# A GRU followed by an expert-choice layer: states in a ring with one gather, another load order, and softmax and late sums arranged anew

## The chip, the core and the metric

The kernel runs on one core of a Trainium2 chip. A core has five engines that work side by side: TensorE (PE) for matmuls, with its weight loads (PEld) shown apart, VectorE (DVE), ScalarE (ACT), GpSimd (POOL) and SyncE (SP). Sixteen DMA engines move data between the large memory (HBM) and the on-chip memory (SBUF). Matmuls write into PSUM, which has eight banks of 128 partitions by 512 float32 values. The metric is the time of one execution on the device in microseconds (us); lower is better.

## The reference

Inputs are `x` (16 x 256 x 512, float32), a start state `cond` (16 x 512), two GRU weight matrices of 512 x 1536 with biases, a router of 512 x 16 and an expert of 512 x 512 with their biases. First a GRU runs over 256 steps, then an expert-choice layer routes each of the 16 x 256 = 4096 tokens, and the result is added to `x`:

```python
def cell(h, x):
    gi = x @ W_ih + b_ih
    gh = h @ W_hh + b_hh
    i_r, i_z, i_n = jnp.split(gi, 3, axis=-1)
    h_r, h_z, h_n = jnp.split(gh, 3, axis=-1)
    r = jax.nn.sigmoid(i_r + h_r)
    z = jax.nn.sigmoid(i_z + h_z)
    n = jnp.tanh(i_n + r * h_n)
    return (1.0 - z) * n + z * h
...
logits = xf @ router_w + router_b          # xf: the GRU's states, 4096 x 512
S = jax.nn.softmax(logits, axis=-1)
G, idx = jax.lax.top_k(S.T, k)             # k = 4096 / 16 = 256 tokens per expert
out = jnp.einsum('ekh,hd->ekd', xf[idx], expert_w) + expert_b
# each token's weighted expert outputs are summed, and x + y is returned
```

All 16 experts share one weight matrix, so a token's result is (state @ expert_w + expert_b) times one number, its gate: the sum of the probabilities with which experts chose it.

## The kernel before, in words

**Units.** Eight steps form a group (`TG = 8`; eight steps of 16 batch rows are 128 tokens), so there are 32 groups (`NG`). Two steps form a pair. A feature vector of 512 is cut into four blocks (`KC = 4`), and a matmul's output into four quadrants of 32 partitions, so a product is issued as four matmuls side by side. The trace counts each float32 matmul twice.

**Head.** Small loads (biases, router bias, start state) and the weights are issued on two queues, SP and ACT, in an order written by hand (L198 to L221, under `manual_schedule`): biases first, then `xa0` (x of group 0), the start state `c0`, then `wih` r and n, `whh` r and n, `wih` z, `whh` z, each in two halves of 512 KB, one on each queue, then `xa1` (x of group 1), the expert and router weights `ewr`, the expert bias `eb` and the router bias `rb`. PE first zeroes six PSUM banks (`begin_sums`, L119) and adds the biases (L236); then come the x products of pair 0 (`x_part`, L337): `ra` holds r and the x side of n, `zz` holds z, `hn` the state side of n, each in two copies for alternate pairs. DVE turns x around (`turn_x`, L190).

**Recurrence.** For the 256 steps the order on all five engines is the written one (L372). In a step PE adds the state products for r, n and z (`h_part`, L350), then part of the x products of the next pair (three of four blocks of `ra` in an even step, the last block and all of `zz` in an odd one). ACT takes the sigmoid of r (L407), the two tanh halves (L428) and the sigmoid of z (L429); DVE multiplies and adds (L424, L426), transposes n and z (L433, L436), and forms the new state in two halves: `less_n` (L439), `by_z` (L444), `plus_n` (L447). States go into `hs`, which has a place for each of the 257. After a group, POOL copies its states into token order (`gather`, L267, into `tok`, two buffers). For every second group PE then computes logits and expert sums in small units between the steps (`expert`, L303), and DVE adds the bias and writes the sums over the states of that group in `hs` (`expert_done`, L320). For the 17 others (`late_groups`) only the logits are computed in the recurrence (`logits`, L280). Logits less their maximum go into `lg` (`less_max`, L273, L274). POOL also makes two small copies a step or fewer (L106, L472), which hold back the SP queue's next loads of x until a step is reached.

**Tail.** After the last group's logits: exp, sum, reciprocal and product over all groups (L546 to L550), four transposes on PE (L556), a copy (L560), then a search for each expert's 256th largest probability in 30 bits: DVE compares and counts (L572), PE adds the counts (L577), DVE sets the bit (L580, L583). PE fills its time with the late groups' expert sums (`expert_for`, L519), two or three of 136 parts a bit. For a late group POOL gathers the states again (`late_begin`, L498), ACT writes the bias into a PSUM bank (L503), PE adds eight parts, and ACT copies the sums over the group's states (L531). After the search come ranks among equals (L594 to L630), the gates (L633, L635), and for each of the 32 groups one DVE operation, x plus gate times sums (L641), and a 256 KB store on SP (L644); the late groups are last.

## Time and profile before

Three runs took 1204.85, 1210.37 and 1207.17 us; their median is 1207.17 us.

| what | value |
|---|---|
| median of three runs | 1207.17 us |
| the profiled execution's own time | 1206.09 us |
| its span, first to last instruction | 1204.2 us |
| mean granted TensorE clock | 0.993 |
| PE, PEld, DVE, ACT, POOL busy | 96%, 86%, 58%, 27%, 11% |
| moved by DMA | 38.05 MB, of it 28.90 MB on the busiest queue |
| first step's r sigmoid | at 28.61 us |
| step 1's first state product | at 30.95 us |
| last step's state complete | at about 1108.4 us |
| search begins, ends | at 1116.7, 1161.2 us |
| gates ready, first output product | at 1169.5 us |
| last output product begins | at 1199.8 us |

Times in the profile count from the span's start. A line of a group, such as those quoted in the prediction, names the line of the kernel, the engine, the operation, the tile written and the tiles read, the shapes and the number of instructions; in a list in order of time the first column is the start and the second the length, and in brackets stands how long the engine had been idle and what released it. A line of the table by stage has the stretch, its length, the busy time of each engine with its instruction count, the granted clock (1.00 is full), the DMA engines' busy share and what they moved in GB/s. A line of waits names who waited for whom, the total in us, how often, and the longest.

### The profile page before, as it was taken

Reading aid. Unit: us, or ns where it says so; the run is one execution under the profiler, and the core shown is the slowest. Engines: PE = TensorE matmul, PEld = TensorE weight load, DVE = VectorE, ACT = ScalarE, POOL = GpSimd, SP = SyncE. Lnnn points to the kernel's source line nnn. Section 1 sums busy time; section 2 is a strip of 40 time slices with the busy share of each in tenths; the row PEclk is TensorE's granted clock in tenths of the full one; section 3 lists DMA queues with packets and bytes.
Section 4 is the critical chain, followed back from the end, with each engine's and each line's share of the span. In section 5 each row is a group of like instructions: output and inputs, shape, how many; then the busy total and the mean of one; then the engine's idle time right before and its main releaser. Section 6 shows DMA issues by size and latency. Waiting matters only on the chain.

```text
span 1204.2 us, 80862 instructions
## 1 busy us (share of the span) xinstructions
PE 1161.5 (96%) x36482; PEld 1041.2 (86%) x36482; DVE 703.2 (58%) x3915; ACT 327.6 (27%) x1440; POOL 131.7 (11%) x458
## 2 busy tenths in 40 slices
PE   4999999999999999999999999999999999998896
PEld 3899999999999899999999999999999999996443
DVE  1555655565555655565655655555655655565685
ACT  0223232222222222222322222222222232223221
POOL 0000000000000000000000000000000000002235
PEclk9999999999999999999999999999999999999998
DMA  7100000000000000000000000000000000000007
GB/s 260 36 21 21 20 18 22 19 20 20 20 22 20 20 19 20 20 22 20 20 21 19 20 20 19 20 22 20 18 22 20 20 19 21 20 11 8 2 29 253
DMA packets 48833, 38.05 MB, mean 32 GB/s; under 512 B 7909, under 2 KB 40677, under 8 KB 48488
## 3 DMA queue, kind: packets, MB, share of 16 engines
q1 hardware_dynamic: 45364, 28.90, 8.1%
q8 instruction: 285, 4.67, 1.5%
q10 hardware_dynamic: 3124, 3.98, 1.0%
q14 instruction: 60, 0.49, 0.1%
HBM read 24.47 MB, written 8.39 MB: 27 GB/s over the span
## 4 chain that ended last, share of the span: by engine, by line
PE 88%; DVE 6%; DMA 2%; POOL 1%; issue 1%; ACT 1%; ACTq 0%; DVEq 0%; POOLq 0%
PE ra L350 19%; PE hn L350 19%; PE zz L350 17%; PE ra L337 16%; PE zz L337 9%; PE pe L303 4%; PE pe L519 3%; POOL tok L498 1%; DVE ge L572 1%; DVE nT L433 1%; DMA whh<-in_L_cond_W_hh_dram 1%; DVE t L424 1%; DMA xa<-in_x_dram 1%; DVE zT L436 1%; ACT n L428 1%
## 5 line engine op out<-in xcount | busy, mean ns | idle before, releaser
L350 PE MATMUL ra<-whh,hs 128*16 128x128 f32 (+1 forms) x8192 | 338.2, 273 | 6.5 <-DVE zT L436 5.1
L350 PE MATMUL hn<-whh,hs 128*16 128x128 f32 (+1 forms) x8192 | 337.5, 273 | 0.8 <-DMA whh<-in_L_cond_W_hh_dram 0.8
L424 DVE TENSOR_TENSOR t<-r,hn 128x64 f32<-128x64 f32 x512 | 90.5, 218 | 370.3 <-PE hn L350 349.2
L337 PE MATMUL ra<-wih,xt 128*32 128x256 f32 x4096 | 281.9, 381 | 5.8 <-DMA wih<-in_L_cond_W_ih_dram 4.4
L350 PE MATMUL zz<-whh,hs 128*16 128x128 f32 (+1 forms) x8192 | 281.4, 273 | 2.2 <-DMA whh<-in_L_cond_W_hh_dram 1.8
L350 PEld LDWEIGHTS ra<-whh,hs 128*16 128x16 f32 (+1 forms) x8192 | 237.2, 103 | 18.6 <-issue 7.6
L350 PEld LDWEIGHTS hn<-whh,hs 128*16 128x16 f32 (+1 forms) x8192 | 249.9, 103 | 1.4 <-DMA whh<-in_L_cond_W_hh_dram 1.3
L350 PEld LDWEIGHTS zz<-whh,hs 128*16 128x16 f32 (+1 forms) x8192 | 235.8, 103 | 4.2 <-DMA whh<-in_L_cond_W_hh_dram 2.1
L407 ACT ACTIVATE r<-ra 128x128 f32<-128x128 f32 x256 | 71.2, 278 | 580.1 <-PE ra L350 580.1
L337 PEld LDWEIGHTS ra<-wih,xt 128*32 128x32 f32 x4096 | 149.5, 110 | 41.1 <-issue 9.6
L428 ACT ACTIVATE n<-t 128x64 f32<-128x64 f32 x512 | 104.1, 250 | 192.9 <-DVE t L426 192.6
L337 PE MATMUL zz<-wih,xt 128*32 128x128 f32 x4096 | 142.6, 273 | 1.7 <-DMA wih<-in_L_cond_W_ih_dram 1.2
L337 PEld LDWEIGHTS zz<-wih,xt 128*32 128x32 f32 x4096 | 125.7, 110 | 18.4 <-issue 2.4
L433 DVE STREAM_TRANSPOSE nT<-n 128x64 f32<-128x64 f32 x512 | 100.8, 235 | 57.5 <-ACT n L428 57.2
L436 DVE STREAM_TRANSPOSE zT<-zs 128x64 f32<-128x64 f32 x512 | 122.0, 238 | 0.9 <-ACT zs L429 0.6
L447 DVE TENSOR_TENSOR hs<-v,nT 128x32 f32<-128x32 f32 x512 | 102.1, 199 | 17.5
L444 DVE TENSOR_TENSOR v<-u,zT 128x32 f32<-128x32 f32 x512 | 105.7, 206 | 8.8
L303 PE MATMUL pe<-ewr,tok 128*32 128x136 f32 (+1 forms) x1920 | 103.0, 276 | 0.0
L426 DVE TENSOR_TENSOR t<-t,ra 128x64 f32<-128x64 f32 x512 | 88.9, 216 | 0.1
L303 PEld LDWEIGHTS pe<-ewr,tok 128*32 128x32 f32 x1920 | 70.9, 110 | 12.8
L439 DVE TENSOR_TENSOR u<-hs,nT 128x32 f32<-128x32 f32 x512 | 78.6, 154 | 0.0
L519 PE MATMUL pe<-ewr,tok 128*32 128x256 f32 x1088 | 71.2, 406 | 5.3 <-POOL tok L498 5.3
(100 smaller groups left out, 553.4 us busy)
## 6 DMA issues: line engine op xcount, KB each, us to landing
xs<-in_x_dram SPq DMA_DIRECT2D x128, 64.0 KB, 2.2
out_dram<-xs SPq DMA_DIRECT2D x32, 256.0 KB, 3.6
xa<-in_x_dram SPq DMA_DIRECT2D x248, 32.0 KB, 2.2
wih<-in_L_cond_W_ih_dram ACTq DMA_DIRECT2D x3, 512.0 KB
wih<-in_L_cond_W_ih_dram SPq DMA_DIRECT2D x3, 512.0 KB
whh<-in_L_cond_W_hh_dram ACTq DMA_DIRECT2D x3, 512.0 KB, 11.5
whh<-in_L_cond_W_hh_dram SPq DMA_DIRECT2D x3, 512.0 KB, 12.2
ewr<-in_L_ffn_expert_w_dram ACTq DMA_DIRECT2D x1, 512.0 KB, 4.0
```

What stands on the lines that cost most here:

```text
L303: nc.tensor.matmul(pe[quadrant(j), at : at + w], toks[g][:, k, quadrant(j)], ewr[:, k, src : src + w], start=(k == 0), stop=(k == KC - 1), ...
L337: nc.tensor.matmul(dst, lhs, rhs, start=False, stop=(k == KC - 1), tile_position=(0, QD * j), skip_group_check=True)
L350: nc.tensor.matmul(dst[quadrant(j, m)], lhs, columns(whh[:, k, slot, :], j), start=False, stop=(k == KC - 1), tile_position=(0, QD * j), s ...
L424: nc.vector.tensor_tensor(t[half], r[:, cols], hn[p % 2][:, cols], ALU.mult)
L426: nc.vector.tensor_tensor(t[half], t[half], ra[p % 2][:, 1, cols], ALU.add)
L428: nc.scalar.activation(n[half], t[half], AF.Tanh)
L433: nc.vector.transpose(nT[half], n[half])
L436: nc.vector.transpose(zT[half], zs[:, halves[half][1]])
L439: nc.vector.tensor_tensor(u[half], hs[:, halves[half][2], s, :], of_step(nT[half], odd), ALU.subtract)
L444: nc.vector.tensor_tensor(v[half], u[half], of_step(zT[half], odd), ALU.mult)
L447: nc.vector.tensor_tensor(hs[:, halves[half][2], s + 1, :], v[half], of_step(nT[half], odd), ALU.add)
L519: nc.tensor.matmul(pe[q, cols], tok[:, k, q], ewr[:, k, E:][:, cols], start=False, stop=(k == KC - 1), tile_position=(0, QD * j), skip_gro ...
```

## The change

- **States in a ring.** `hs` shrinks to the start state and 16 places, used in turn (`slot`). A new tile `ht` holds the token order of all 32 groups; `gather` writes into it once, and the logits, the expert units and the late sums all read it. Expert sums are written over a group's part of `ht` (`wide`).
- **Head.** Biases, router bias and the start state are loaded from POOL's queue. SP and ACT begin with `wih` r, then `xa0`, `wih` n, `wih` z, then all of `whh`. `xa1` and everything after it goes on SP alone. The x products of pairs 0 and 1 are all issued before step 0, so steps 0 and 1 issue none.
- **Softmax.** exp, sum, reciprocal and product of groups 0 to 30 are issued before those of group 31. The fourth transpose goes into a bank of its own, and its copy is DVE's.
- **Late sums.** The first two late groups' banks are begun in steps 250 and 252, the others after the fifth part of the group two before. Four parts follow the last logits directly. Five banks are used in turn instead of three. Sums that are complete before the gates are copied by ACT as before; later ones are read by the output product from PSUM. PE's remaining parts are issued between the output products instead of ahead of them.

The diff, cut to its core (`late_part` is the body of L519's matmuls with `ht` in place of `tok`; in the remaining places `toks` becomes `ht` and `s` becomes `slot(s)`):

```diff
--- before.py
+++ after.py
@@ -60,12 +64,13 @@
     const = ctx.enter_context(tc.tile_pool(name="const", bufs=1))

     xs = const.tile([P, NG, D], F32, name="xs")
-    hs = const.tile([P, KC, T + 1, B], F32, name="hs")
+    ht = const.tile([P, NG, KC, P], F32, name="ht")
     HD = D // 2
...
+    tot = const.tile([P, NG], F32, name="tot")
...
-    def load_x(g, j, s):
-
-        cols = slice(j * P, (j + 1) * P)
-        nc.gpsimd.tensor_copy(xs[0:1, g, cols][:, 0:1], hs[0:1, 0, s, 0:1])
-        nc.sync.dma_start(out=xs[:, g, cols], in_=x[:, g * TG : (g + 1) * TG, cols])
-
-    def expert_out(g):
-        return hs[:, :, g * TG + 1 : (g + 1) * TG + 1, :].rearrange("p k t b -> p k (t b)")
-
-    def blocks(ap):
-        return ap.rearrange("p (k d) -> p k d", d=P)
...
+    def wide(g):
+
+        return ht[:, g, :, :].rearrange("p k d -> p (k d)")
+
+    ps_m = ctx.enter_context(tc.tile_pool(name="ps_m", bufs=2, space=bass.MemoryType.PSUM))
+
...
+    late = []
+    late_sums = {}
+    late_done = []
+    gated = []
+
+    def late_begin(pool, fresh=True):
+        g = late_groups[len(late_done) + len(late)]
+        pe = pool.tile([P, D], F32, name="pe", tag="pe")
+        if fresh:
+            begin_sums(pe)
+        nc.scalar.copy(pe, eb)
+        late.append((g, pe))
+
+    def late_parts():
+        for i, g in enumerate(late_groups):
+            _, pe = late[0]
+            for part in range(2 * KC):
+                late_part(g, pe, part)
+                if part == KC and i + 2 < len(late_groups):
+                    n = (i + 2) % 5
+                    late_begin(ps_m if n < 2 else late_pool[0], fresh=i < 3)
+                if part == 2 * KC - 1:
+                    late.pop(0)
+                    late_done.append(g)
+                    if gated:
+                        late_sums[g] = pe
+                    else:
+                        nc.scalar.copy(wide(g), pe)
+                yield
...
-        tc.tile_pool(name="toks", bufs=2) as tp,
+        tc.tile_pool(name="states", bufs=1) as sp,
         tc.tile_pool(name="ps_g", bufs=1, space=bass.MemoryType.PSUM) as ps_g,
-        tc.tile_pool(name="ps_m", bufs=1, space=bass.MemoryType.PSUM) as ps_m,
+        hs = sp.tile([P, KC, 2 * TG + 1, B], F32, name="hs")
+
+        def slot(s):
+            return 1 + (s - 1) % (2 * TG) if s else 0
...
         queues = (nc.sync, nc.scalar)
         ET = mybir.EngineType
         xa0 = new_xa()
+        for dst, src in (
+            (b_raw[0:1], b_ih.rearrange("(o g d) -> o g d", o=1, d=D)),
+            (b_raw[1:2], b_hh.rearrange("(o g d) -> o g d", o=1, d=D)),
+            (b_n, b_hh[2 * D :].rearrange("(o d) -> o d", o=1)),
+            (b_r, router_b.rearrange("(o e) -> o e", o=1)),
+        ):
+            nc.gpsimd.dma_start(out=dst, in_=src)
+        for j in range(KC):
+            nc.gpsimd.dma_start(
+                out=c0[QD * j : QD * j + B, :].rearrange("b (c i) -> b c i", c=KC), in_=columns(cond, j)
+            )
+        xa1 = new_xa()
         with tc.manual_schedule(engines={ET.SP, ET.Activation}):
-            for h, src in enumerate((b_ih, b_hh)):
-                queues[h].dma_start(out=b_raw[h : h + 1], in_=src.rearrange("(o g d) -> o g d", o=1, d=D))
-            nc.sync.dma_start(out=b_n, in_=b_hh[2 * D :].rearrange("(o d) -> o d", o=1))
-            nc.scalar.dma_start(out=b_r, in_=router_b.rearrange("(o e) -> o e", o=1))
+            for i, gate in enumerate((0, 2, 1)):
+                load_rows(wih[:, :, i, :], w_ih[:, gate * D : (gate + 1) * D], "(p c) n -> p c n")
+                if i == 0:
+                    for j in range(KC):
+                        load_xa(0, xa0, j, queues)
+            for gate in (0, 2, 1):
+                load_rows(whh[:, :, gate, :], w_hh[:, gate * D : (gate + 1) * D], "(c p) n -> p c n")
             for j in range(KC):
-                load_xa(0, xa0, j, queues)
-            for j in range(KC):
-                queues[j % 2].dma_start(
-                    out=c0[QD * j : QD * j + B, :].rearrange("b (c i) -> b c i", c=KC), in_=columns(cond, j)
-                )
-            for slot, gate in enumerate((0, 2, 1)):
-                if slot == 2:
-                    for h_gate in (0, 2):
-                        load_rows(whh[:, :, h_gate, :], w_hh[:, h_gate * D : (h_gate + 1) * D], "(c p) n -> p c n")
-                load_rows(wih[:, :, slot, :], w_ih[:, gate * D : (gate + 1) * D], "(p c) n -> p c n")
-            load_rows(whh[:, :, 1, :], w_hh[:, D : 2 * D], "(c p) n -> p c n")
-            xa1 = new_xa()
-            for j in range(KC):
-                load_xa(1, xa1, j, queues)
-            load_rows(ewr[:, :, E:], expert_w, "(c p) n -> p c n")
-            load_rows(ewr[:, :, 0:E], router_w, "(c p) n -> p c n")
+                load_xa(1, xa1, j, (nc.sync, nc.sync))
+            nc.sync.dma_start(out=ewr[:, :, E:], in_=expert_w.rearrange("(c p) n -> p c n", c=KC))
+            nc.sync.dma_start(out=ewr[:, :, 0:E], in_=router_w.rearrange("(c p) n -> p c n", c=KC))
             nc.sync.dma_start(out=eb, in_=expert_b.rearrange("(o d) -> o d", o=1).to_broadcast([P, D]))
-            nc.scalar.dma_start(out=rb, in_=router_b.rearrange("(o e) -> o e", o=1).to_broadcast([P, E]))
+            nc.sync.dma_start(out=rb, in_=router_b.rearrange("(o e) -> o e", o=1).to_broadcast([P, E]))
...
         def gather(g):

-            toks[g] = tp.tile([P, KC, P], F32, name="tok")
             n = TG - 1 if g == NG - 1 else TG
+            at = slot(g * TG + 1)
             for k in range(KC):
                 nc.gpsimd.tensor_copy(
-                    toks[g][:, k, :].rearrange("p (b t) -> p b t", t=TG)[:, :, 0:n], tokens(g, k)[:, :, 0:n]
+                    ht[:, g, k, :].rearrange("p (b t) -> p b t", t=TG)[:, :, 0:n],
+                    hs[:, k, at : at + n, :].rearrange("p t b -> p b t"),
                 )
...
-                pes[g] = [ps_m.tile([P, n], F32, name=f"pe{n}") for n in (E + HD, HD)]
+                pes[g] = [ps_m.tile([P, D], F32, name="pe", tag="pe")[:, 0:n] for n in (E + HD, HD)]
...
-                out_h = expert_out(g)[:, KC // 2 * h : KC // 2 * (h + 1), :]
-                nc.vector.tensor_tensor(out_h, blocks(pe if h else pe[:, E:]), blocks(eb[:, d]), ALU.add)
+                nc.vector.tensor_tensor(wide(g)[:, d], pe if h else pe[:, E:], eb[:, d], ALU.add)
...
-                lhs = hs[:, k, s - odd : s + 1, :].rearrange("p t b -> p (t b)")
+                lhs = hs[:, k, slot(s) - odd : slot(s) + 1, :].rearrange("p t b -> p (t b)")
...
-        for k in range(KC):
-            x_part(0, k, False)
+        for z in (False, True):
+            for p in range(2):
+                for k in range(KC):
+                    x_part(p, k, z)
...
-                if s == 0:
-                    for k in range(KC):
-                        x_part(0, k, True)
                 h_part(s, "z", range(KC))
...
-                if s + 2 < T:
+                if 2 <= s < T - 2:
...
-                        hs[:, halves[half][2], s + 1, :], v[half], of_step(nT[half], odd), ALU.add
+                        hs[:, halves[half][2], slot(s + 1), :], v[half], of_step(nT[half], odd), ALU.add
...
+                if s in (T - 6, T - 4):
+                    late_begin(ps_m)
+
+
+            old, new = slice(0, NG - 1), slice(NG - 1, NG)
+
+            def softmax(gs):
+                nc.vector.reciprocal(tot[:, gs], tot[:, gs])
+                n = gs.stop - gs.start
+                nc.vector.tensor_tensor(
+                    lg[:, :, gs], lg[:, :, gs], tot[:, gs].unsqueeze(1).to_broadcast([P, E, n]), ALU.mult
+                )
+
+            def exp_sum(gs):
+                nc.scalar.activation(lg[:, :, gs], lg[:, :, gs], AF.Exp)
+                nc.vector.tensor_reduce(tot[:, gs], lg[:, :, gs].rearrange("p e g -> p g e"), AX.X, ALU.add)
+
             nc.vector.tensor_copy(
-                toks[NG - 1].rearrange("p k (b t) -> p k b t", t=TG)[:, :, :, TG - 1], hs[:, :, T, :]
+                ht[:, NG - 1, :, :].rearrange("p k (b t) -> p k b t", t=TG)[:, :, :, TG - 1], hs[:, :, slot(T), :]
             )
             logits(NG - 1, hn[(T // 2) % 2][:, P:])
+            expert_for(4)
+            exp_sum(old)
             less_max(NG - 1, hn[(T // 2) % 2][:, P:])
+            softmax(old)
+            exp_sum(new)
+            softmax(new)
...
-        def late_begin(g):
-
-
-            tok = lt.tile([P, KC, P], F32, name="tok")
-            for k in range(KC):
-                nc.gpsimd.tensor_copy(
-                    tok[:, k, :].rearrange("p (b t) -> p b t", t=TG),
-                    hs[:, k, g * TG + 1 : (g + 1) * TG + 1, :].rearrange("p t b -> p b t"),
-                )
-            pe = ps_e.tile([P, D], F32, name="pe")
-            nc.scalar.copy(pe, eb)
-            return tok, pe
...
-
-            for _ in range(3):
-                begin_sums(ps_e.tile([P, D], F32, name="pe"))
-            ready = [late_begin(g) for g in late_groups[:2]]
-            for i, g in enumerate(late_groups):
-                tok, pe = ready.pop(0)
...
-                    if part == 3 and i + 2 < len(late_groups):
-                        ready.append(late_begin(late_groups[i + 2]))
-                    if part == 2 * KC - 1:
-                        nc.scalar.copy(expert_out(g), blocks(pe))
-                    yield g
...
+        late_pool.append(ps_e)
...
-        sm = rt.tile([P, E, NG], F32, name="sm")
-        nc.scalar.activation(sm, lg, AF.Exp)
-        tot = rt.tile([P, NG], F32, name="tot")
-        nc.vector.tensor_reduce(tot, sm.rearrange("p e g -> p g e"), AX.X, ALU.add)
-        nc.vector.reciprocal(tot, tot)
-        nc.vector.tensor_tensor(sm, sm, tot.unsqueeze(1).to_broadcast([P, E, NG]), ALU.mult)
-
-        expert_for(4)
         ps = ps_s.tile([P, QG, P], F32, name="ps", tag="s")
-        sm_f = sm.rearrange("p e g -> p (e g)")
-        for q in range(QG):
-            nc.tensor.transpose(ps[:, q, :], sm_f[:, q :: QG], ident)
+        ps_last = ps_n.tile([P, P], F32, name="ps_last", tag="n")
+        lg_f = lg.rearrange("p e g -> p (e g)")
         sT = rt.tile([P, QG * P], F32, name="sT")
+        for q in range(QG - 1):
+            nc.tensor.transpose(ps[:, q, :], lg_f[:, q :: QG], ident)
+        nc.tensor.transpose(ps_last, lg_f[:, QG - 1 :: QG], ident)
         by_row = lambda ap: ap.rearrange("p (q b t) -> p b q t", q=QG, b=B)
         by_step = lambda ap: ap.rearrange("p b (q t) -> p b q t", q=QG)
-        nc.scalar.copy(sT, ps.rearrange("p q n -> p (q n)"))
+        nc.scalar.copy(sT[:, 0 : (QG - 1) * P], ps[:, 0 : QG - 1, :].rearrange("p q n -> p (q n)"))
+        nc.vector.tensor_copy(sT[:, (QG - 1) * P :], ps_last)
...
-        expert_for(len(late_groups) * KC * 2)
+        gated.append(True)
         for g in [g for g in range(NG) if g not in late_groups] + late_groups:
+            while g in late_groups and g not in late_done:
+                expert_for(1)
             nc.vector.scalar_tensor_tensor(
-                blocks(xs[:, g, :]), expert_out(g), gate[:, g : g + 1], blocks(xs[:, g, :]), ALU.mult, ALU.add
+                xs[:, g, :], late_sums.get(g, wide(g)), gate[:, g : g + 1], xs[:, g, :], ALU.mult, ALU.add
```

## The prediction

> **What bounds the kernel now.** I read the page's busy shares first, then a table of busy time by stage, then each stage that is not steady in order of time, with the chain of waits beside it. The page and the stage table (us, busy time by engine, granted clock, DMA share, GB/s):
>
> ```profile
> PE 1161.5 (96%) x36482; PEld 1041.2 (86%) x36482; DVE 703.2 (58%) x3915; ACT 327.6 (27%) x1440; POOL 131.7 (11%) x458
> ...
> 0.00:31.00 31.00, 14.41 (x292) 10.13 (x296) 6.17 (x29) 2.13 (x5) 1.91 (x14) 1.00 0.77 259
> 31.00:1103.00 1072.00, 1066.07 (x34920) 988.56 (x34920) 628.76 (x3692) 302.21 (x1394) 88.05 (x371) 1.00 0.07 20
> ...
> 1117.00:1161.00 44.00, 39.81 (x622) 19.03 (x625) 32.53 (x119) 10.61 (x18) 12.83 (x36) 1.00 0.01 2
> 1161.00:1169.00 8.00, 7.26 (x107) 4.34 (x100) 7.27 (x18) 2.35 (x4) 3.68 (x8) 1.00 0.01 3
> 1169.00:1204.00 35.00, 24.66 (x378) 13.32 (x378) 21.66 (x33) 5.30 (x9) 17.83 (x8) 0.85 0.74 241
> ```
>
> PE is busy 1066 of the recurrence's 1072 us. The diff takes no matmul out of steps 2 to 255, so this block stays; what can move is 31 us of head and 101 of tail. Head, in order of time, and the SP queue's own waits:
>
> ```profile
> 16.93 8.68 ACTq L180 DMA_DIRECT2D xa<-in_x_dram  x4
> 26.07 1.07 PE L350 MATMUL zz<-whh,hs 128*16 128x128 f32 x32 [1.79 <-DMA whh<-in_L_cond_W_hh_dram]
> 27.31 1.28 ACT L407 ACT_TABLE_LOAD   x1 [27.31 <-DMA xa<-in_x_dram]
> 30.95 0.65 PE L350 MATMUL ra<-whh,hs 128*32 128x128 f32 x16 [2.52 <-DVE zT L436]
> ...
> SPq L180 <- DMA whh<-in_L_cond_W_hh_dram: 7.0, 3, 2.5
> SPq L172 <- DMA wih<-in_L_cond_W_ih_dram: 6.5, 2, 3.9
> SPq L180 <- DMA wih<-in_L_cond_W_ih_dram: 2.4, 1, 2.4
> SPq L180 <- DMA xs<-in_L_cond_b_ih_dram: 0.7, 1, 0.7
> ```
>
> Two things end the head: the last weights (z of whh) at 26.07, and ACT, which still issues xa1 and later loads until 27.3, so that step 0's sigmoid comes at 28.6 and step 1 at 30.95. The four waits fit one reading: over both queues, in written order, a load waits for the one eight places before it (xa0's third pair for b_ih; z of wih for r of wih; the four pairs of xa1 for whh r, whh n, wih z, whh z). Tail:
>
> ```profile
> 1111.63 3.64 PE L519 MATMUL pe<-ewr,tok 128*32 128x256 f32 x32
> 1116.68 0.75 DVE L572 TENSOR_SCALAR_CACHE_REDUCE ge<-sT,cand 128x512 bf16<-128x512 f32 x1 [3.74 <-ACT sT L560]
> ...
> 1169.53 19.96 DVE L641 SCALAR_TENSOR_TENSOR xs<-hs,gate,xs 128x512 f32<-128x512 f32 x30
> 1174.27 17.83 POOL L498 COPY tok<-hs 128x128 f32<-128x128 f32 x8 [5.60 <-PE pe L519]
> 1189.80 9.19 PE L519 MATMUL pe<-ewr,tok 128*32 128x256 f32 x128 [5.33 <-POOL tok L498]
> 1199.77 0.75 DVE L641 SCALAR_TENSOR_TENSOR xs<-hs,gate,xs 128x512 f32<-128x512 f32 x1 [2.73 <-ACT hs L531]
> ...
> 1194.00:1196.00 2.00, 2.00 (x40) 1.08 (x36) 0.00 (x0) 0.33 (x1) 0.00 (x0) 0.98 1.00 348
> 1196.00:1198.00 2.00, 2.00 (x44) 1.12 (x40) 0.75 (x1) 0.26 (x1) 0.00 (x0) 1.00 0.10 37
> ```
>
> At the end eight POOL gathers take 17.8 us (one alone 15.48) while DVE runs the 30 output steps; PE waits for them, the last two groups come at 1196.3 and 1199.8, and the DMA engines, full until 1196, fall to 0.10. So the output is bound by DMA for 30 groups and by the gathers for the last two.
>
> **The change part by part.** The sum is made against the profiled execution: span 1204.2, its own time 1206.09 (1.9 around the span). The median of the three runs is 1207.17, so 1.08 is added at the end.
>
> *Head.* New order on SP and ACT: wih r (places 0, 1), xa0 (2 to 9), wih n, wih z, whh r, n, z; all of xa1 and the later loads on SP alone. Wih r goes out at 0.74 instead of 5.2. It lands 4.1 to 5.3 us after its issue now (the loads that wait for it go out at 9.31 and 10.78), so at 4.9 to 6.0. By the rule of eight, xa0's last pair (places 8, 9) must wait for that, and wih n stands behind it on both queues: issue at about 6.3, with 1.25 MB alone in flight before, which leaves the engines a gap of 2 us. From there five MB: now six take 20.7 us from first issue to sight (26.07 less 5.4), and one is 2.7 to 2.9 (20.48, 23.19, 26.07 for the last three), so 17.9, and whh z is there at 24.2. Its matmuls take 1.07 and from the z sigmoid to step 1's first matmul it is 1.20 (29.75 to 30.95): step 1 at 26.5, gain 4.4. ACT's last issue waits for wih n, near 11.5, so its table load is done by 14 and hides. SP's eight xa1 issues, ewr, eb and rb end near 26; x of group 1 is needed at step 3, ewr at step 8 (30 us later), so nothing waits.
>
> The x products of pair 1 move from steps 0 and 1 into the head. They save nothing in step 1, which DVE bounds (30.95 to 35.04, with the next `ra` held by L447). In the head PE must do biases 3.9 (6.86 to 10.7), pair 0's `ra` 3.64 (15.15), pair 1's at full rate 1.74 (8 matmuls in 0.43), both z 2.2: 11.4 in all, from DVE's `ones`, which stand behind xa0's transpose (8.4 landing + 1.1): 9.5 to 20.9, before whh n at 21.4. Cover 0.5, plus 1.5 that the n side has on z; later biases cost one for one beyond 2 us.
>
> No row shows a DMA on POOL. Bounds: SP's small issues at 0.22 to 0.43 us with 2.1 to landing, against the Trainium skill, "DMA: Bandwidth & Descriptors", specifications, first byte about 1 us from GpSimd and 0.6 from SP or ACT. Four bias loads from 2.15 (POOL's last memset) land at 5 to 8.3, the four of the state at 7 to 12.3; I take 6.5 and 9, nearer the rows. Both are hidden. The same page ("Issuing engines are not separate DMA queues") speaks against the edit: spreading loads over engines saves only issue time, small beside the transfer. The trace disagrees here: between 2 and 6 us the DMA share is 0.15 to 0.48 and both queues issue without a break. By the rule whh z would still come at 26.07 and only ACT's early release count: step 1 at 28.3 (26.07 + 1.07 + 1.20), gain 2.6; by the row 4.4. I take the row, and keep 2 to 6.
>
> *Recurrence.* The gathers were all made once already (128 copies, L267) and only change their target; `expert_done` writes the same sizes. L444 to L447 gain one thing: a state overwrites a slot that POOL read up to 15 steps before. That event lies 60 us back, and the wait stands on an instruction that has none: zT of half 0 also waits on ACT and starts 0.07 after `u`, the same pace. Cost 0; bounds in the rivals. If POOL were late, DVE's second half and PE's next `ra` would queue behind it; its gather ends 1.6 us into a step, eight steps ahead. Two `begin_sums` (1.47 for three, cold) enter steps 250 and 252: at most 0.3 in all; their ACT copies (0.59) fit in the 1.7 us that ACT waits for `ra`.
>
> *Before the search.* Now: logits end at 1109.55, zeroing 1.47, four parts 3.6, transposes 0.8, copy 0.6, search at 1116.68. After: the parts follow the logits directly (1109.6 to 1113.1, same cold clock), transposes to 1113.95, the split copy 0.3 more: 1114.3. Gain 2.4. DVE is not late: reduce 1.04 from 1108.8 (table load and exp end by 1108.6), max and subtract 0.45, reciprocal 0.35, product 0.73, the new group's three small ones 0.6: 1112.0. Should PE get its full clock, 1112 becomes the bound.
>
> *Search.* Three zeroings move here: in bits with three parts (PE 1.48 of 1.47) they cost 0.25 to 0.5, in bits with two nothing: +0.6. POOL's copies go; they stretch L583 from 160 to 186 ns on average, 29 times: -0.5 of 0.76, as PE bounds half the bits. The clock: it is 0.50 from 1109.0 to 1115.5 and 1.00 from the search on. By that row, nothing. But the Trainium skill, "TensorE: Matmul & The Clock Gate", Part 1, says a free-running window of about 3.4 us must be busy before the clock rises; now 3.5 us of parts and 0.8 of transposes lie before a pause of 1.1, where zeroing and parts made 5.8. By the rule two or three bits may run cold, each three-part one 1.2 longer: 0 to 3. I take +1.2.
>
> *After the search.* `at_least` (0.93) runs beside a POOL copy, others of its kind 0.67 to 0.75: -0.3.
>
> *Output.* First bytes come 2.0 after the gates (1169.5 to 1171.5). 30 groups, 7.86 MB, went in 24.4 us, 322 GB/s; 32 need 26.1; data end 1197.8, plus the 1.2 that now lies between the last data and the end: 1199.0 against 1204.2, gain 5.2. Hidden under it: DVE 32 x 0.67; PE's 47 parts, seven cold in 4.9 and 40 at 0.43, to 1191.4. Six groups are read from PSUM (89 parts are done at the gates, 11 groups, which ACT copies as before); group 16 reuses the bank of group 11, free after DVE's 27th step at 1187.5, copy 0.6, eight parts 3.5, last product 1192.4; DMA reaches it at 1196.7. Cover 4; the ACT copies saved are worth nothing there.
>
> Sum: -4.4 +0.3 -2.4 +0.6 -0.5 +1.2 -0.3 -5.2 = -10.7: 1195.4 for a run like the profiled, 1196.5 beside the median.
>
> **The rivals.** *A: the head keeps its length.* POOL's loads count among the eight places, or land after 13 us: PE then ends its x products past 24. For it: no row; against: 3 us of cover. Gain 0.5: 1200.4. *B: the output stays late.* Bank reuse behind DVE and a cold PE (0.54 at 1170 to 1172) hold the last groups past 1196.7; this takes 4 us, 40 parts at 0.53. Gain 2: 1199.7. *C, slower: the ring's wait costs a step of DVE's queue.* An instruction with two waits shows 0.10 ahead of it in the chain (37.02 to 37.12). On 254 steps 25 us, net 1222; break-even at 0.042 per step, or 0.084 if only every second step, the one that DVE bounds, pays. Against: one wait, not two. That the change does less than it says: only six of 17 late sums stay in PSUM; counted.
>
> **How the numbers follow.** Main 0.72 (1196.5; own range 1191.5 to 1200.5: head 2 to 6, search 0 to 3, output 4 to 6); A 0.15; B 0.08; C 0.05. Within 0.5% (6 us, about what a measurement here can tell from no change) are two fifths of A and B. Faster 0.86, same 0.09, slower 0.05. The range, 1191 to 1201.5, leaves out C, the ends of the main case and part of A.
>
> **What would show it.** Step 1's first `ra` at 26 to 27 and ACT's table load before 15 (A: past 29); whh z's wait ending near 24; pairs without expert units still 8.2 us (C: 8.3 to 8.4); search 2.4 earlier after the recurrence, its first bits longer than 1.5; no POOL copy after it; DMA full without a break for 26 us, and the last product 4 us ahead of the last data. A pair that grows, or biases after 11.5, would prove me wrong.

## The result, and the profile after

The changed kernel takes 1205.6 us (median of 20 runs, 1200.8 to 1209.1), the kernel before 1211.7 on the same chips (20 runs, 1204.9 to 1216.2): ratio 0.9947, 95% interval 0.9933 to 0.9961. The forecast was 1196.5, with a range to 1201.5. It is faster by 0.5%, 6 us where 10.7 were worked out, and from a base that was itself 4.5 too low: the three runs of before that were at hand (median 1207.17) lay in the lower half of what it does. The profiled execution of the changed kernel took 1205.67 (span 1203.9).

Of the page and of a table by stage (us, busy time of PE, PEld, DVE, ACT, POOL, granted clock, DMA share, GB/s):

```profile
PE 1163.5 (97%) x36490; PEld 1052.9 (87%) x36490; DVE 699.1 (58%) x3919; ACT 323.3 (27%) x1435; POOL 96.0 (8%) x398
...
0.00:31.00 31.00, 17.12 (x364) 12.29 (x368) 6.14 (x30) 2.24 (x5) 6.04 (x22) 0.96 0.71 236
...
1119.00:1165.00 46.00, 41.88 (x628) 19.72 (x626) 32.18 (x120) 10.97 (x20) 0.00 (x0) 0.96 0.01 2
...
1173.00:1204.00 31.00, 21.95 (x372) 12.43 (x364) 21.25 (x32) 0.72 (x2) 0.00 (x0) 0.87 0.84 273
```

POOL has no copy left in the search and the output, and the output takes 31 us in place of 34.7 with the DMA engines at 0.84. The head has more PE work (17.1 against 14.4) at a clock of 0.96. In order of time, with the SP queue's own waits and the clock of step 1:

```profile
3.42 0.48 ACTq L228 DMA_DIRECT2D wih<-in_L_cond_W_ih_dram  x1
...
16.41 1.28 ACT L465 ACT_TABLE_LOAD   x1 [16.41 <-DMA wih<-in_L_cond_W_ih_dram]
26.85 1.07 PE L409 MATMUL zz<-whh,hs 128*16 128x128 f32 x32 [1.86 <-DMA whh<-in_L_cond_W_hh_dram]
29.14 1.08 PE L409 MATMUL ra<-whh,hs 128*32 128x128 f32 x16 [1.22 <-DVE zT L494]
34.66 0.61 PE L409 MATMUL ra<-whh,hs 128*16 128x128 f32 x13 [1.26 <-DVE hs L505]
...
SPq L228 <- DVE row_of L106: 2.7, 1, 2.7
...
30.00:31.00 1.00, 1.00 (x25) 1.00 (x20) 0.00 (x0) 0.00 (x0) 0.00 (x0) 0.50 0.94 326
```

W_ih goes out at 3.42, not at 0.74: both queues wait 2.7 us for DVE's last mask operation, because `wih` was given the memory that the masks had just left. Whh z is seen at 26.85, and step 1 starts at 29.14 (forecast 26.5; before 30.95). Then step 1 runs at half clock (1.08 for 16 matmuls; before 0.65), so that step 2 starts at 34.66, where before it was 35.04. The tail:

```profile
1190.90 0.59 ACT L156 COPY pe<-eb 128x512 f32<-128x512 f32 x1 [17.77 <-DVE xs L670]
1191.54 5.35 PE L136 MATMUL pe<-ewr,ht 128*32 128x256 f32 x64 [1.95 <-ACT pe L156]
...
1197.01 0.75 DVE L670 SCALAR_TENSOR_TENSOR xs<-pe,gate,xs 128x512 f32<-128x512 f32 x1 [3.51 <-issue]
```

Rival B's mechanism is there (group 16's bank comes free behind DVE's steps, PE stands 1.95 and goes on at half clock), but the last product at 1197 is still ahead of the stores, whose last data move near 1202.

By stage, from all profiles taken (four of before, two of after; step times by the start of `r`'s sigmoid):

| us | before | after | mean change | forecast |
|---|---|---|---|---|
| to step 3 | 40.79, 43.57, 41.25, 41.27 | 40.40, 41.86 | -0.6 | -4.4 |
| steps 16 to 250, at the medians of the 16 kinds of step | 979.5, 979.6, 979.4, 979.4 | 980.8, 980.8 | +1.3 | 0 |
| the same steps, above those medians | 10.2, 14.5, 16.9, 16.0 | 15.7, 17.2 | scatter (+2.1) | 0 |
| step 255 to the end of the search | 56.2, 55.1, 55.6, 55.6 | 53.2, 52.7 | -2.7 | -1.1 |
| after the search | 8.3 | 7.2 | -1.1 | -0.3 |
| output | 34.75, 29.96, 34.54, 34.62 | 31.04, 30.62 | -2.6 | -5.2 |

A kind of step is its place in two groups (16 steps). Without the scatter the rows make -5.7, near the -6.1 of the runs' medians; six profiles are too few to price the scatter, and the head's row hangs on one profile of before (43.57).

### The profile page after: what moved, and what is told of

It is laid out like the page before. It is cut to its first block, busy times and chain, and to the rows that moved or that the text cites. A ratio compares the mean times of both kernels' runs of the same rounds, so it can differ in the third digit from the quotient of the medians.

```text
span 1203.9 us, 80849 instructions
## 1 busy us (share of the span) xinstructions
PE 1163.5 (97%) x36490; PEld 1052.9 (87%) x36490; DVE 699.1 (58%) x3919; ACT 323.3 (27%) x1435; POOL 96.0 (8%) x398
## 5 line engine op out<-in xcount | busy, mean ns | idle before, releaser
L409 PE MATMUL ra<-whh,hs 128*16 128x128 f32 (+1 forms) x8192 | 348.4, 274 | 6.9 <-DVE zT L494 4.9
L409 PE MATMUL hn<-whh,hs 128*16 128x128 f32 (+1 forms) x8192 | 348.1, 273 | 0.8 <-DMA whh<-in_L_cond_W_hh_dram 0.8
L396 PE MATMUL ra<-wih,xt 128*32 128x256 f32 x4096 | 288.4, 381 | 5.1 <-DMA wih<-in_L_cond_W_ih_dram 3.2
L409 PE MATMUL zz<-whh,hs 128*16 128x128 f32 (+1 forms) x8192 | 288.2, 273 | 3.0 <-DMA whh<-in_L_cond_W_hh_dram 1.9
L409 PEld LDWEIGHTS hn<-whh,hs 128*16 128x16 f32 (+1 forms) x8192 | 259.7, 104 | 1.2 <-DMA whh<-in_L_cond_W_hh_dram 1.1
L409 PEld LDWEIGHTS ra<-whh,hs 128*16 128x16 f32 (+1 forms) x8192 | 246.3, 103 | 15.5 <-issue 5.9
L396 PEld LDWEIGHTS ra<-wih,xt 128*32 128x32 f32 x4096 | 158.9, 110 | 38.3 <-issue 11.6
L396 PEld LDWEIGHTS zz<-wih,xt 128*32 128x32 f32 x4096 | 129.0, 110 | 17.1 <-issue 5.0
L505 DVE TENSOR_TENSOR hs<-v,nT 128x32 f32<-128x32 f32 x512 | 101.9, 199 | 21.7
L363 PE MATMUL pe<-ewr,ht 128*32 128x136 f32 (+1 forms) x1920 | 108.2, 276 | 0.0
L363 PEld LDWEIGHTS pe<-ewr,ht 128*32 128x32 f32 x1920 | 76.5, 110 | 10.9 <-issue 0.5
L136 PE MATMUL pe<-ewr,ht 128*32 128x256 f32 x1088 | 69.5, 395 | 1.9 <-ACT pe L156 1.9
```

Of the source, the lines that this page charges most:

```text
L363: nc.tensor.matmul(pe[quadrant(j), at : at + w], ht[:, g, k, quadrant(j)], ewr[:, k, src : src + w], start=(k == 0), stop=(k == KC - 1), t ...
L396: nc.tensor.matmul(dst, lhs, rhs, start=False, stop=(k == KC - 1), tile_position=(0, QD * j), skip_group_check=True)
L409: nc.tensor.matmul(dst[quadrant(j, m)], lhs, columns(whh[:, k, gate_, :], j), start=False, stop=(k == KC - 1), tile_position=(0, QD * j), ...
L505: nc.vector.tensor_tensor(hs[:, halves[half][2], slot(s + 1), :], v[half], of_step(nT[half], odd), ALU.add)
```

## The experiments

Times are medians; each ratio is to the kernel before, run beside it. "Step 3" is the start of its first sigmoid.

**after_again**, the changed kernel unaltered.

> The changed kernel unaltered, for a second profiled execution. If the recurrence's +6.6 us (steps 2 to 248: 1039.3 before, 1045.9 after) is mostly gaps in the instruction supply that differ from one execution to the next, this profile shows another number for it, anywhere from 1040 to 1048, while the steps that begin a group of 8 stay at 4.24 us in the middle. If it is the change's own, it shows 1045 to 1047 again. Step 2's first ra at 34.7 either way.

1205.9, ratio 0.9937 (0.9916 to 0.9958). Steps 2 to 248 took 1047.6, the steps that begin a group 4.245 in the middle. That alone does not tell the two readings apart; the further profiles of before do (below): supply differs between executions, and the 4.245 is the change's own. Step 1 was cold (at half clock) for twice as long (step 2's `ra` at 36.1), which I had not expected: the head of this kernel varies.

**wih_early**

```diff
+        tc.tile_pool(name="states", bufs=1) as sp,
         tc.tile_pool(name="wts", bufs=1) as wts,
...
-        tc.tile_pool(name="states", bufs=1) as sp,
```

> The ring of states is allocated ahead of the weights, so that it, and not w_ih, takes the memory of the masks. Theory (w_ih's first load waits at 3.42 for DVE's last mask operation because it reuses that memory): both queues issue w_ih r at 0.74, everything behind it comes 2.7 us earlier, whh z is seen at 24.2 and step 1's first ra at 26.4 to 26.6, time -2.7 us against the changed kernel. Rival (the small loads of POOL, or the eight places of the queues, set the pace): w_ih r goes out early, but xa0 or the biases land no earlier, whh z stays at 26 to 27, time within 0.5 us.

```profile
0.75 0.45 SPq L228 DMA_DIRECT2D wih<-in_L_cond_W_ih_dram  x1
23.55 1.30 PE L409 MATMUL zz<-whh,hs 128*16 128x128 f32 x32 [1.24 <-DMA whh<-in_L_cond_W_hh_dram]
32.27 0.51 PE L409 MATMUL hn<-whh,hs 128*16 128x128 f32 x10 [0.40 <-issue]
```

The theory holds in the trace: W_ih at 0.75, whh z at 23.55, step 1's `ra` at 26.07, step 3 at 36.7 in place of 40.4. In the time it is not clear of noise: 1203.8, ratio 0.9930 (0.9904 to 0.9957), 1.8 to 2.1 below the changed kernel's two medians, with intervals that overlap; the steps 2 to 248 of its profile took 1051.2, the longest of all. (DVE does the masks behind xa0's transpose here; one wait of 0.38 us, for a weight load at 11.73, is put down to them.)

**x_back**

```diff
         for z in (False, True):
-            for p in range(2):
-                for k in range(KC):
-                    x_part(p, k, z)
+            for k in range(KC):
+                x_part(0, k, z)
...
-                if 2 <= s < T - 2:
+                if s < T - 2:
```

> Pair 1's x products go back from the head into steps 0 and 1. Theory (PE stands still in step 0 without them and its clock falls to 0.50 for step 1, whose matmuls then take 1.08 us for 16 in place of 0.65): clock 1.00 from 29 to 32 us, step 1 to step 2 takes 4.1 us in place of 5.5, time -1.4 us; the head to step 1 keeps its length, since whh z still ends it at 26.9. Rival (step 1 is slow because DVE or ACT is late, or the products cost what they save): step 1 to 2 stays above 5, time within 0.4 us.

```profile
30.00:31.00 1.00, 1.00 (x47) 1.00 (x40) 0.17 (x1) 0.00 (x0) 0.00 (x0) 1.00 0.74 186
...
37.19 0.51 PE L409 MATMUL hn<-whh,hs 128*16 128x128 f32 x10 [1.69 <-issue]
```

Clock and step 1 are as the theory says (1.00; 4.02 us), yet the time stays: 1205.9, ratio 0.9952 (0.9931 to 0.9972). Nor does this profile show that the products are what keeps the clock: of the five profiles whose head up to step 1 is the changed kernel's, after, after_again and sums_copied run step 1 at half clock, ring_touch and softmax_late do not; and x_back_ewr, with the products back, is at half clock from 22.9 to 29.7. In step 2 PE now stands still 1.69 us for nothing that the profile shows, and step 3 comes at 41.6. The page has a DMA queue that carries PE's program:

```profile
q8 instruction: 286, 4.69, 1.6%
```

286 packets of 16 KB, one for every 256 PE instructions (matmuls and weight loads) in the steady part. The trace gives each packet's times. The third, against PE's instruction count when it started:

| kernel | starts | at PE instruction | landed | PE's stop in step 2 ends |
|---|---|---|---|---|
| before | 32.73 | 712 | 33.61 | none |
| after | 33.05 | 844 | 33.99 | none |
| wih_early | 29.93 | 848 | 30.92 | 32.27 |
| x_back | 34.51 | 908 | 35.79 | 37.19 |
| ring_touch | 34.35 | 900 | 35.27 | 36.64 |
| softmax_late | 34.59 | 884 | 35.61 | 36.85 |
| x_back_ewr | 32.45 | 724 | 33.70 | none |

Each stop is at PE instruction 953 or just behind it and ends 1.24 to 1.40 after the packet landed. From 31 to 34 us the DMA engines of x_back are full (share 1.02 to 1.07), the expert weights among it. The cold step 1 of the changed kernel had only hidden that: cold or not, step 3 comes at 40.4, 41.9 and 41.0 (after, after_again, sums_copied) and at 41.0 and 41.2 (ring_touch, softmax_late, which have the stop).

**x_back_ewr**, as x_back, and in the loop over steps:

```diff
-            nc.sync.dma_start(out=ewr[:, :, E:], in_=expert_w.rearrange("(c p) n -> p c n", c=KC))
...
+                if 2 <= s <= 2 + KC:
+                    load_ewr(s - 2)
```

(`load_ewr(i)` loads 128 rows of `expert_w` for i under 4, then the router's weights and both biases.)

> As x_back (pair 1's products back in steps 0 and 1), and the 1.3 MB of expert and router weights and their biases, which SP issues at 28.6 to 30.1, are issued in pieces in steps 2 to 6 instead. Theory (a packet of PE's instructions stands behind these loads in the DMA engines: in x_back it began at PE instruction 908 in place of about 730, landed at 35.8, and PE stood still from 35.4 to 37.2): the third packet begins by PE instruction 780, PE's gap of 1.69 us in step 2 is gone, step 2 to 3 takes 4.2 us in place of 6.2, and the time falls 1.5 to 2.0 against x_back. Rival (PE's gap is a fixed cost of the code's place, or of the loads of x that remain): a gap of over 1 us stays at PE instruction 953, time within 0.5 us of x_back.

The packet starts at instruction 724 and the stop is gone (step 2 takes 4.17). So that stop was the packet behind the bulk loads, which the trace shows. The time, 1203.7, ratio 0.9925 (0.9896 to 0.9954), is 2.2 below x_back's, but the intervals overlap.

**ring_touch**

```diff
+                if c == TG - 1 and 2 * TG - 2 < s < T - 1:
+                    nc.vector.memset(hs[:, :, slot(s + 2), 0:1], 0.0)
```

> A DVE write of one column into the slot that the next group's first state will take, put at the end of the step before, where DVE has 1.5 us to spare: it takes over the wait for POOL's gather. Theory (the ring costs 0.067 us in each of the two writes of a state that are first to reuse what a gather read, 30 of 254 steps): those steps fall from 4.242 to 4.175 and 4.207 us in the middle, time -1.4 to -1.6 us. Rival (the ring is free, the recurrence's growth is supply gaps alone): no step changes, time within 0.3 us. Rival 2 (the ring costs more than seen, in every step): -3 us or more.

DVE's rows of the changed kernel in a step that begins a group, then in one that does not:

```profile
503.62 0.19 DVE L502 TENSOR_TENSOR v<-u,zT 128x32 f32<-128x32 f32 x1
503.91 0.19 DVE L505 TENSOR_TENSOR hs<-v,nT 128x32 f32<-128x32 f32 x1
...
512.15 0.19 DVE L502 TENSOR_TENSOR v<-u,zT 128x32 f32<-128x32 f32 x1
512.38 0.19 DVE L505 TENSOR_TENSOR hs<-v,nT 128x32 f32<-128x32 f32 x1
```

And in ring_touch, in a step that begins a group:

```profile
506.43 0.19 DVE L502 TENSOR_TENSOR v<-u,zT 128x32 f32<-128x32 f32 x1
506.65 0.19 DVE L505 TENSOR_TENSOR hs<-v,nT 128x32 f32<-128x32 f32 x1
```

0.29 from `v` to the state in the first, 0.23 in the second, and that for both halves; 0.22 to 0.23 in ring_touch. With the column written ahead, the two kinds of step fall from 4.242 and 4.242 to 4.175 and 4.207, exactly the values of before; 15 of each make 1.5 us. The time fell more than that, to 1202.7, ratio 0.9921 (0.9891 to 0.9950), but this interval overlaps the changed kernel's and takes in 1.5, and no other kind of step changed.

**head_old**, the changed kernel with the head of before (loads and x products).

```diff
-                load_rows(wih[:, :, i, :], w_ih[:, gate * D : (gate + 1) * D], "(p c) n -> p c n")
-                if i == 0:
-                    for j in range(KC):
-                        load_xa(0, xa0, j, queues)
...
+            for h, src in enumerate((b_ih, b_hh)):
+                queues[h].dma_start(out=b_raw[h : h + 1], in_=src.rearrange("(o g d) -> o g d", o=1, d=D))
...
```

> The changed kernel with the head of the kernel before (biases and state on the SP and ACT queues, xa0 first, z of w_ih behind whh, later loads on both queues, x products of pair 0 alone in the head). Theory (the new head gains next to nothing until step 3: 40.4 to 41.9 against 40.8): time within 0.7 us of the changed kernel, step 3's sigmoid at 40.8. Rival (the new head is worth what it gains at step 1, 1.8 us, and the profiles at hand were unlucky): 1.5 to 2 us slower than the changed kernel.

1207.2, ratio 0.9959 (0.9945 to 0.9972), step 3 at 43.2 where the theory had 40.8: like before_again it was cold in step 1. The new head is worth 1.2 to 1.6 by the medians, more than the 0.6 of the profiles; the intervals overlap. Between the two expectations.

**before_again, before_p3, before_p4**, the kernel before unaltered.

> The kernel before, unaltered, for a second profiled execution. Theory (gaps in PE's instruction supply differ between executions, and the first profile of the kernel before, 1206.1 against a median of 1211.7, had few of them): steps 2 to 248 take 1042 to 1048 us here in place of 1039.3, the middle of each of the 16 kinds of step is unchanged to 0.01 us, head (step 2's sigmoid at 36.6) and tail (99.2) within 0.5 of the first profile. Rival (the recurrence of the kernel before is 6 us shorter whatever the execution): 1038 to 1040 again.

> A third profiled execution of the kernel before, unaltered. Theory (POOL's gathers stall beside DVE's output steps in most executions; the kernel with the gathers ahead has a tail of 98.7 us and the time of the kernel before, so the latter's tail must be near 98.7 too): one gather of over 5 us, output stage 33 to 36, tail 98 to 100. Rival (the stall is the exception): output stage 29.5 to 31, tail 93 to 94. Either way the recurrence from step 2 to 248 takes 1040 to 1048.

> A fourth profiled execution of the kernel before, unaltered, with the same expectations as the third: with theory, a gather of over 5 us and an output stage of 33 to 36; with the rival, 29.5 to 31.

POOL's gathers from 1160 us on, in before_p3 and in before_again (shortest, middle and longest in ns):

```profile
L498 POOL COPY tok<-hs x23: 388/402/15470, 1159.8 to 1198.1; 128x128 f32<-128x128 f32 x23
```

```profile
L498 POOL COPY tok<-hs x24: 396/434/880, 1160.5 to 1185.5; 128x128 f32<-128x128 f32 x24
```

Three of four executions have one gather of 15.5 us and an output of 34.5 to 34.8; before_again has none over 0.9 and an output of 30.0, the bare stores. So the row behind my output term is the kernel's usual case, as the theory of before_p3 and before_p4 has it (tails 98.4 and 98.5). The recurrence was the unusual thing in the first profile: 1039.3 for steps 2 to 248, against 1043.5, 1045.8 and 1044.8, with the middles of the kinds of step unchanged. That is the theory of before_again; its other part failed, since its head and tail did not stay within 0.5 (step 2 at 39.4 for 36.6, tail 93.3 for 99.2).

**before_ahead**, an edit of the kernel before

```diff
-        tc.tile_pool(name="late", bufs=4) as lt,
+        tc.tile_pool(name="late", bufs=8) as lt,
...
+            toks_ready = [late_gather(g) for g in late_groups[:6]]
...
+                    if part == 3 and i + 6 < len(late_groups):
+                        toks_ready.append(late_gather(late_groups[i + 6]))
```

> The kernel before with one thing moved: POOL's gathers for the late groups run six groups ahead instead of two (eight buffers in place of four), so that all are done before the output stage. Theory (in most executions of the kernel before, POOL's gathers stall beside DVE's output steps, as in its first profile, where one took 15.5 us and the stage 34.7; its second profile, with a stage of 30.0, is the exception): no POOL copy after the gates, output stage 30 to 31.5 us in every execution, time 3 to 4.5 us below the kernel before. Rival (the stall of the first profile was the exception): 0 to 1 us below, and this part of the change was worth nothing.

Output 29.6 and no POOL copy in it, yet 1210.9, ratio 0.9995 (0.9975 to 1.0015). The time is the rival's, but not for its reason: the copies now lie ahead of and in the search, where the stretch to it takes 15.1 (11.1 in the middle of the four profiles of before) and the search 46.8 (44.5), so that the tail is 98.7. In this profile moving the gathers inside the tail only moved their cost; the changed kernel has none there.

**sums_copied**

```diff
-        gated.append(True)
```

> The changed kernel with the late sums copied out of PSUM by ACT to the end, as before, instead of read in place after the gates. By the prediction the copies saved were worth nothing: time within 0.4 us, output stage 30 to 31.5. Theory now: the same, or a little better, since a bank comes free after ACT's copy and no longer waits for DVE's 27th step (PE stood 1.95 us for it and fell to half its clock at 1190): the last product 2 to 4 us earlier, hidden under the stores. Rival (reading the sums in place is what keeps the end short): 1 us or more slower.

1206.4, ratio 0.9947 (0.9927 to 0.9967), 0.5 to 0.8 above the changed kernel's medians and not told from them; the output takes 31.3, the last product is done 21.7 after the gates in place of 24.9, and no gain follows from it. As predicted.

**softmax_late**

```diff
-            exp_sum(old)
             less_max(NG - 1, hn[(T // 2) % 2][:, P:])
-            softmax(old)
-            exp_sum(new)
-            softmax(new)
+            exp_sum(slice(0, NG))
+            softmax(slice(0, NG))
```

> The changed kernel with one softmax over all 32 groups after the last logits, in place of 31 groups ahead of them. From step 255 to the search it is 7.3 us now and was 11.6 or 10.6 before. By the durations of the profile (reduce 1.03, reciprocal 0.34, product 0.68, exp 0.62 behind the last maximum at 1117.4 in place of mostly ahead of it) the transposes start at 1120.4 in place of 1118.5: the stretch to the search takes 9.2, time +1.5 to +2.0. Rival (the parts of the late sums on PE, or the clock, bound this stretch, not DVE): under +0.7.

8.8 to the search in place of 7.3 and 8.1. The half-clock stretch falls ahead of the search or in it and shifts time between the two (7.3 and 45.8 us in after, 8.1 and 44.6 in after_again), so the sum is the better measure: 54.7 from step 255 to the search's end, in place of 53.2 and 52.7. 1208.1, ratio 0.9965 (0.9949 to 0.9981), 2.2 to 2.5 slower by the medians, of which this stretch shows 1.5 to 1.9. The theory holds: DVE's softmax is on the path.

**best**, wih_early, x_back, ring_touch and the later expert weights together; **best_xa**, the first edit below to it; **best_pool**, the second in place of that load.

```diff
-                if i == 0:
+                if i == 1:
                     for j in range(KC):
                         load_xa(0, xa0, j, queues)
```

```diff
+        for j in range(KC):
+            load_xa(0, xa0, j, (nc.gpsimd, nc.gpsimd))
```

> The changed kernel with all four edits: the ring ahead of w_ih in memory, pair 1's x products back in steps 0 and 1, the column written to take over the ring's wait, the expert weights loaded in steps 2 to 6. Theory: the head's gain is delivered (step 3's sigmoid at 35.5 to 36.5 against 40.4 in the changed kernel's profile), the recurrence loses its 1.5 us of waits: 5.5 to 6.5 us below the changed kernel, 1199 to 1200.5 us in the middle. Rival (the next packet of instructions is late instead, since PE now gets to it earlier, or the pieces of the expert weights delay others): a new gap of 1 us or more in steps 3 to 8, total 3 to 4 us below the changed kernel.

> The version with all four edits, and xa0 issued behind w_ih r and n instead of between them. Theory (a load waits for the one eight places ahead in written order over both queues: xa0's last pair for w_ih r, and the 5 MB behind it with it, which leaves the DMA engines a gap of some 2 us): w_ih n goes out at 1.3, the gap is gone, whh z is seen at 22 to 22.5 in place of 24.1, step 3's sigmoid at 34.5 in place of 36.2, time -1.5 us against the version with four edits. Rival (PE's own work in the head, x products behind a later xa0, or instruction packets end the head): step 3 at 35.5 or later, time within 0.5 us.

> The version with all four edits, and xa0 issued by POOL, between the biases and the state, so that the SP and ACT queues carry nothing but the six weights until whh z. Theory (a load waits for the one eight places ahead over the SP and ACT queues: with xa0 among them the DMA engines idle for 2 us before w_ih n, at 6 to 8 us with xa0 second and at 8.5 to 12 with xa0 third): no pause in the weights, 6.3 MB at 385 GB/s from 2.5 us, whh z seen at 19.5 to 20.5 in place of 24.1, step 3's sigmoid at 32.5 to 34 in place of 36.2, time -2 to -3.5 us against the version with four edits. Rival (xa0 now lands late, behind the weights, at 14 or later, and PE's x products end the head; or an instruction packet behind the weights does): step 3 at 35 to 36.5, within 0.7 us.

| kernel | time | ratio | w_ih n out | whh z seen | step 3 |
|---|---|---|---|---|---|
| best | 1201.9 | 0.9912 (0.9881 to 0.9942) | 6.8 | 24.1 | 36.2 |
| best_xa | 1201.4 | 0.9901 (0.9872 to 0.9930) | 1.3 | 24.9 | 37.2 |
| best_pool | 1200.2 | 0.9906 (0.9874 to 0.9938) | 1.2 | no wait | 37.8 |

In best the head comes as its theory has it, but the time is 3.7 to 4.0 below the changed kernel's, the rival's sum, without the rival's gap (no step from 3 to 8 is more than 0.31 us over its usual length). The DMA share and rate (last two columns) of best, then of best_pool, and what POOL and PE wait for in the latter:

```profile
6.00:8.00 2.00, 0.00 (x0) 0.00 (x0) 0.00 (x0) 0.00 (x0) 0.24 (x1) 1.00 0.45 79
```

```profile
6.00:8.00 2.00, 0.00 (x0) 0.00 (x0) 0.00 (x0) 0.00 (x0) 0.25 (x1) 1.00 1.06 388
...
8.24 1.52 POOL L236 DMA_DIRECT2D xa<-in_x_dram  x3 [1.99 <-DMA xs<-in_L_cond_b_ih_dram]
18.27 3.64 PE L399 MATMUL ra<-wih,xt 128*32 128x256 f32 x32 [5.93 <-DVE xt L252]
```

In best_xa the pause only moved, to some 9 to 12 us, since w_ih z now stood behind xa0's last pairs. In best_pool it is gone and no matmul waits for a weight, but POOL's queue shows the same wait: xa0's fifth load waits 1.99 us for b_ih, the load eight places before it, the last goes out at 10.0, each takes 5.1 to 6.8 to land beside the weights, and PE's x products start at 18.3. So the eight places do cost the 2 us that the prediction saw, and both cures were met by the next wait, xa0, as the rivals have it. By time the three are not told from one another. They lie 4 to 6 us below the changed kernel's medians; the interval of best_xa lies clear of the changed kernel's first one (0.9933 to 0.9961) and overlaps after_again's.

## Why the prediction was off

- *The base.* Three runs of before gave 1207.2; all twenty gave 1211.7, and the sets beside the experiments 1211.5 to 1212.5. That is 4.5 of the miss of 9.1; I added 1.08 to the profiled execution where about 5.6 belonged.
- *The head: the failed step is "Wih r goes out at 0.74 instead of 5.2".* It went out at 3.42. The wait comes from a memory address, and was covered before by the biases, xa0 and the state, which the change moved off these queues or behind this load. wih_early shows it. Everything behind it up to step 1 came out as reckoned, 2.7 later: the eight places, the pause of 2 us, whh z at 26.85 for 24.2 (23.6 once the start is early), step 1 at 29.14 for 26.5 (26.1), a gain of 1.8 there in place of 4.4. The 28.3 that the prediction worked out from the rule it set aside is nearer to 29.14, but by luck: with the early start alone step 1 comes at 26.1, as by the row that it took.
- *"They save nothing in step 1".* True of the work. The clock was left out: with pauses of 1.9 and 1.2 us around whh z, PE is at half speed in step 1, 1.4 us or more. That the missing products are the reason is argued, not shown: two profiles with the same head keep the clock, and before_again and head_old lose it in step 1 with the products there. Nor did it cost time up to step 3, since behind it stands the next brake, the packet of instructions: curing the first alone gave nothing, both together about 2 by the medians, with intervals that overlap.
- *"Cost 0" for the ring: the mis-sized term is 1.4 to 1.5 us.* Rival C had the right mechanism. What saved the forecast from it is the number of steps, 30 of 254: only the first state that reuses what a gather read carries the wait. It is about 0.067 in each half, and the step grows by 0.067 or, in every second group, by 0.035. "A pair that grows" was a sign of being wrong, and these pairs grew.
- *Zeroing in steps 250 and 252*: at most 0.3 was allowed; both take 4.19 in after_again, head_old and ring_touch against 4.18 in the first profile of before, so it is hidden. (Single executions have 4.2 to 4.7 in one of the two, before as well as after.)
- *Before and in the search*: -1.1 reckoned, -2.7 found, as the clock was full at the parts (in the profile of before that was used: half). The cold 3.41 us fell into the search in after (45.8 us; before 44.5) and just ahead of it in after_again (44.6), so that the 1.2 set down for cold bits came in one of two.
- *After the search*: -0.3 reckoned, -1.1 found. In all four profiles of before a POOL gather ran beside the four products ahead of the gates:

```profile
1166.85 1.83 POOL L498 COPY tok<-hs 128x128 f32<-128x128 f32 x4 [2.60 <-PE pe L519]
1167.23 1.59 DVE L630 TENSOR_TENSOR at_least<-rank,at_least 128x128 f32<-128x128 f32 x4
```

  Without it they take 0.90 together (L657 after, from 1171.22), and so they do in before_ahead, which is the kernel before with no gather at that place: 7.2 after the search there too.
- *Output: the right mechanism, too large.* 3.5 to 4.1 in place of 5.2 against the usual case: the stores ran at 310 and 315 GB/s, not 322, and 1.9 lies after them, not 1.2. (The sum had a slip, too: 1171.5 and 26.1 make 1197.6, not 1197.8.) The whole tail was forecast at -6.6 and came to -6.4 in the mean, by luck: two terms were 1.6 and 0.8 too small, one 2.6 too large.

So the tail's sum came true by errors that cancel, the head was short by 3 to 4, the ring 1.4 wrong, the base 4.5 too low. Not settled: why the head of before, too, sometimes takes 3 us longer (step 3 at 43.6 in before_again, its step 1 cold), and why the runs with an early start gain less time than their traces gain by step 3.

## What to carry to other kernels

Where a load is moved to the front, ask what held its destination last: the wait sits in the allocator's addresses and shows only once the cover is gone. One profile is one execution: price a term from a row that a second profile repeats, and set the base on more than three runs. At the start of a kernel the PE's own program shares the DMA engines with the weights, so loads not needed yet belong behind the first steps (here they held PE for up to 1.69 us).

## What was not expected of the hardware

- *PE's program comes by DMA and can be late.* In the recurrence, too, the stops put down to "issue" end shortly after a packet lands: in the changed kernel at 525.02 (landed 523.60), 678.84 (677.62), 730.32 (728.83), 840.22 (838.69), so 1.2 to 1.5 later. Such stops come in every profile, and most of the 10 to 19 us above the medians goes with them: in the changed kernel's first profile 41 of 234 steps run over 0.1 us late, 15.0 us together, and 30 of these, 13.0 us, hold a stop of PE or its weight loads of over 0.15 us put down to "issue"; of the other 193 steps 17 do (first profile of before: 8.1 of 10.1 us). That a packet is behind each was not tried.
- *Half-clock stretches last 3.41 us or two or three times that* in all profiles but for the last one of each. This agrees with the Trainium skill, "TensorE: Matmul & The Clock Gate", Part 1, which has a free-running window of 3413 ns. The length of a pause alone does not decide: the same head was cold after pauses of 1.77, 1.86 and 1.93 us and not after 1.59 and 1.73, but x_back kept the full clock through a pause of 2.00 us, and x_back_ewr lost it with one of 2.00.
- *A gather of 0.4 us can take 15.5.* It ran beside 30 DVE steps of 0.665 that read two operands from SBUF. The Trainium skill, "SBUF — State Buffer", terms, has DVE and GpSimd lock a shared port pair for a whole instruction; the trace shows POOL shut out over some 23 instructions in a row (15.47 by 0.665), in three executions of four. That the port does it was not tried by itself.
